# The projections of a Mamba block as one pipeline over 128 blocks in written order

## The chip, the cores and the metric

The kernel runs on one core of one Trainium2 chip. A core has five engines with queues of their own: TensorE (PE, with its weight loads shown as PEld), VectorE (DVE), ScalarE (ACT), GpSimd (POOL) and SyncE (SP), which issues the transfers between the main memory and the on-chip memories. Matmuls write into PSUM, from which ACT and DVE read. The metric is the time of one execution on the device in microseconds (us); a run gives several times and their median counts. One execution is also recorded by the profiler.

## The reference

Input `x` has 2 sequences of 4096 tokens and 512 channels, so 8192 tokens in all. The result is `x + layernorm(mamba(layernorm(x)))`, and onto that once more `x + layernorm(ffn(layernorm(x)))`. Everything is computed in float32. Cut to what matters here:

```python
proj = einsum('blh,ph->blp', x, in_proj_w)            # 512 -> 2048
h_in, gate = split(proj, 2)
u = silu(conv(h_in, conv_w) + conv_b)                 # causal, 4 taps, each channel for itself
ssm = einsum('bli,pi->blp', u, x_proj_w)              # 1024 -> 128 + 16 + 16
ts, Bm, Cm = split(ssm, [128, 144])
dt = softplus(einsum('blr,ir->bli', ts, dt_proj_w) + dt_proj_b)
dA = exp(dt[..., None] * A);  dBx = (dt * u)[..., None] * Bm[:, :, None, :]
hstates = associative_scan(dA, dBx)                   # over the tokens
y = (einsum('blin,bln->bli', hstates, Cm) + D * u) * silu(gate)
return einsum('bli,hi->blh', y, out_proj_w)
```

The feed-forward part multiplies by two weights that are stored in 4 bits with scales per block of 64 and have a low-rank addition (16); between them stands a ReLU.

## The kernel before

The kernel has two stages. Stage A computes the projections of all tokens and prepares the weights of stage B, and writes everything into tensors in the main memory (names ending in `_d`). Stage B runs the scan, the output projection and the feed-forward part. Its instructions on ACT, SP, PE and POOL stand in the order in which they are written out by hand, with a pace of so many matmuls per scan; DVE's are ordered by the framework's scheduler.

**Precision.** A float32 value is held as a high and a low part in the matmul format (`split`: the cast on ACT, the subtraction on DVE), and `mm3` (L99 to L102) makes one product of three matmuls: high x high, high x low, low x high.

**Stage A.** The tokens go in 16 groups of 512 (`g`); the 1024 inner channels in 8 blocks of 128 (`ib`). In stage A before the change all engines are ordered by the framework's scheduler, which lays out a list per engine ahead of time; a few ties are added by hand (`after`, `pace`, `in_set`). What belongs to one group:

- `load_x`, `norm_x`: four tiles of 128 tokens by 512 channels are loaded into the buffers `xA` (4) and normalized on DVE; `rstd_of` takes the power on POOL.
- `turn_x`: four transposes per tile on PE into a PSUM buffer `tp`, then the high part `xnh` on ACT (L174) and the low part `xnl` on DVE (L175). From group 2 on the parts of the last two tiles are stored to `xg_d`, so that stage B can make their gates.
- `h_block`, once per `ib`: twelve matmuls into a PSUM buffer `pm` (two of them, pool `phA`), a copy `hin` on ACT (L335) with three tokens of the group before in front (`halo`, POOL, L334 and L336), the fourth tap on ACT (L337), the other three taps on DVE (L339). In `rest`: silu on ACT into `u` (L344), and the split `us`.
- `gate_block`: twelve matmuls for 128 tokens by 512 gate channels into a PSUM buffer of the pool `psA` (two, which the products `z` of dt and the preparations also use), silu on ACT into `gs` (L361, two buffers), a store to `g_d`. Groups 0 and 1 make eight of these, the later groups the four of their first two tiles; stage B makes the rest in `gates`, from `xg_d` and `wg_d`.
- `x_proj`, once per `ib`: five matmuls with `us`, three blocks behind `h_block`, the last three at the end of the group. Then `x_out` (splits `ts`, stores C) and, in the next group, `b_out` (turns and stores B).
- dt of a group is made during the next one: `dt_mm` (three matmuls, and the bias on ACT or DVE by turns, L400 and L398) in blocks 0 and 1; `dt_out` after block 1: an activation table load, eight softplus (L308) with their stores to `dd_d`, the stores of `du` = D u (L311), the products dt u on POOL (L313), and a table load back; `q_out` in blocks 5 to 7 (2, 3, 3): four transposes of a product into a PSUM buffer `qt` (pool `ptA`, two, which `tp` also uses), a split into `qs` (two buffers of each part) and two stores to `dT_d`.
- Three preparations of weights (`prep_out`, `prep_ffn`): load, dequantize on DVE with the low-rank product from PE, split on DVE and POOL (L184, L185), two stores.

Ahead of the groups the input weights are loaded and split in one row (`load_w`, L244 to L251): sixteen tiles of the input projection, eight of x_proj, two of dt.

After the last group, dt of group 15 is made alone in a sixteenth turn of the loop with no other projections.

**The order of stage B's start.** Its first units need dt, B, C and q of the first group only; its loads stand on SP in the written order.

## Time and profile before

| what | us |
|---|---|
| median of 3 runs | 4846.12 |
| lowest and highest run | 4838.14, 4855.83 |
| the profiled execution, time | 4849.73 |
| the profiled execution, span | 4847.9 |
| PE busy | 4563.9 (94%) |
| DVE busy | 3836.7 (79%) |
| ACT busy | 3320.0 (68%) |
| POOL busy | 3272.9 (68%) |
| mean granted PE clock | 0.977 |

The span is the time from the first to the last instruction of the profiled execution; busy times are shares of it. Matmuls overlap one another, so PE can be shown busy and still not be at its peak: starts of neighbouring matmuls tell more than durations. Lines name an instruction by engine and line of the program, and by the tile it writes and those it reads; "idle before" is the time that the engine stood before it, and behind the arrow is what ended it. Stage A takes roughly the first 1100 us, stage B the rest.

### The profile page before, as it was taken

What the parts mean: (1) busy time and instruction counts of PE and PEld (TensorE: products, weight loads), DVE (VectorE), ACT (ScalarE), POOL (GpSimd) and SP (SyncE); (2) the same over time, 40 slices, a digit from 0 to 9 for tenths busy, and PEclk for the clock granted to TensorE, in tenths of its full rate; (3) what the DMA queues carried; (4) which work ended last, traced back from release to release, by engine and by line L of the source; (5) the groups of instructions that cost most, each with busy time, mean ns of one, the idle gap of its engine ahead of it and who ended that gap; (6) DMA issues with size and microseconds to landing.
All of it is one profiled execution on the core that took longest, in us unless ns stands there. A gap on an engine that the chain in (4) does not pass through costs nothing.

```text
span 4847.9 us, 85729 instructions
## 1 busy us (share of the span) xinstructions
PE 4563.9 (94%) x26736; PEld 3920.6 (81%) x26736; DVE 3836.7 (79%) x6307; ACT 3320.0 (68%) x7411; POOL 3272.9 (68%) x2327
## 2 busy tenths in 40 slices
PE   8999999977999999999999999999999999999999
PEld 6766676756788888888888888888888888888877
DVE  6666666657787898898989888888989898898931
ACT  5766666776777767777676776667776767676643
POOL 2223323227787888888888878888888888788820
PEclk9999999988999999999999999999999999999999
DMA  6877777666798878878787867787787878878765
GB/s 204 244 220 230 218 219 225 214 190 181 225 252 242 235 216 239 229 225 240 213 250 219 240 181 228 216 237 228 225 239 214 250 218 239 225 226 233 215 216 195
DMA packets 1145393, 1085.15 MB, mean 224 GB/s; under 512 B 147281, under 2 KB 918865, under 8 KB 1144946
## 3 DMA queue, kind: packets, MB, share of 16 engines
q1 hardware_dynamic: 1144946, 1079.68, 76.3%
q8 instruction: 221, 3.62, 0.3%
q14 instruction: 226, 1.85, 0.1%
HBM read 801.99 MB, written 277.36 MB: 223 GB/s over the span
## 4 chain that ended last, share of the span: by engine, by line
PE 72%; DMA 12%; DVE 6%; ACT 4%; issue 2%; SPq 2%; POOL 1%; DVEq 0%; ACTq 0%; POOLq 0%
PE yp L711 16%; PE b L661 8%; PE pu L100 5%; PE pu L101 5%; PE pu L102 5%; PE fa L100 5%; PE fa L101 5%; PE fa L102 5%; DMA ys<-y_d 3%; DMA d<-dT_d 2%; DVE pm L339 2%; PE pm L100 2%; DVE h L679 2%; PE pm L101 2%; PE pm L102 1%
## 5 line engine op out<-in xcount | busy, mean ns | idle before, releaser
L691 POOL TENSOR_TENSOR pr<-h,cb 128x1008 f32<-128x1008 f32 (+1 forms) x1056 | 2451.5, 2333 | 525.6 <-DVE b L678 240.2
L679 DVE TENSOR_TENSOR_SCAN h<-dA,b 128x512 f32<-128x512 f32 x2080 | 2534.9, 1220 | 150.0 <-ACT dA L635 15.4
L635 ACT ACTIVATE dA<-dt,A 128x252 f32<-128x252 f32 (+1 forms) x4352 | 1763.5, 487 | 171.8 <-DVE h L679 150.4
L711 PE MATMUL yp<-ident,pr 128*126 128x128 f32 (+1 forms) x8448 | 1114.4, 276 | 17.9 <-POOL pr L691 7.9
L711 PEld LDWEIGHTS yp<-ident,pr 128*126 128x126 f32 (+1 forms) x8448 | 961.4, 141 | 25.4 <-POOL pr L691 9.3
L661 PEld LDWEIGHTS b<-bd,d 128*128 128x128 f32 x4160 | 759.0, 191 | 202.8 <-DMA d<-dT_d 24.1
L661 PE MATMUL b<-bd,d 128*128 128x256 f32 x4160 | 875.8, 292 | 44.9 <-DMA d<-dT_d 22.3
L995 ACT ACTIVATE pu<-pu,bu 128x512 f32<-128x512 f32 x256 | 168.8, 659 | 680.7 <-PE pu L102 680.6
L339 DVE SCALAR_TENSOR_TENSOR pm<-hin,cw,pm 128x512 f32<-128x512 f32 x384 | 284.9, 750 | 233.7 <-ACT pm L337 218.5
L100 PE MATMUL pu<-xh,wu 128*128 128x512 f32 x960 | 411.3, 428 | 58.9 <-DMA wu<-wu_d 58.9
L100 PE MATMUL fa<-wn,hh 128*128 128x512 f32 x1024 | 421.4, 411 | 0.0
L101 PE MATMUL fa<-wn,hh 128*128 128x512 f32 x1024 | 403.7, 394 | 0.0
L102 PE MATMUL fa<-wn,hl 128*128 128x512 f32 x1024 | 401.2, 392 | 0.0
L678 DVE COPY b<-h 128x8 f32<-128x8 f32 x1536 | 255.0, 166 | 178.4 <-PE b L661 170.4
L101 PE MATMUL pu<-xl,wu 128*128 128x512 f32 x960 | 386.4, 402 | 0.0
L102 PE MATMUL pu<-xh,wu 128*128 128x512 f32 x960 | 384.2, 400 | 0.0
L999 DVE TENSOR_TENSOR hl<-pu,hh 128x512 fp32r<-128x512 f32 x256 | 171.8, 671 | 158.4 <-ACT hh L997 158.4
L559 POOL TENSOR_TENSOR bd<-dl,bp 128x512 fp32r<-128x512 f32 x260 | 270.6, 1051 | 11.1 <-DMA d<-dT_d 11.1
L336 POOL COPY halo<-hin 128x3 f32<-128x3 f32 x128 | 31.8, 249 | 331.8 <-ACT hin L335 331.8
L313 POOL TENSOR_TENSOR v<-v,u 128x512 f32<-128x512 f32 x128 | 167.9, 1343 | 124.9 <-DMA dd_d<-v 86.2
L100 PEld LDWEIGHTS pu<-xh,wu 128*128 128x128 f32 x960 | 184.9, 193 | 79.0 <-DMA wu<-wu_d 57.4
L102 PEld LDWEIGHTS fa<-wn,hl 128*128 128x128 f32 x1024 | 192.3, 188 | 44.9 <-DVE hl L999 0.6
(554 smaller groups left out, 7825.1 us busy)
## 6 DMA issues: line engine op xcount, KB each, us to landing
d<-dT_d SPq DMA_DIRECT2D x1024, 128.0 KB
wu<-wu_d SPq DMA_DIRECT2D x256, 512.0 KB
wn<-wn_d SPq DMA_DIRECT2D x256, 512.0 KB
cb<-C_d SPq DMA_DIRECT2D x128, 512.0 KB
wo<-wo_d SPq DMA_DIRECT2D x128, 512.0 KB
dd_d<-du SPq DMA_DIRECT2D x128, 256.0 KB
dd_d<-v SPq DMA_DIRECT2D x128, 256.0 KB
ys<-y_d SPq DMA_DIRECT2D x128, 256.0 KB
```

Of the source, the lines that this page charges most:

```text
L100: nc.tensor.matmul(ps, ah, bh, start=start, stop=False)
L101: nc.tensor.matmul(ps, ah, bl, start=False, stop=False)
L102: return nc.tensor.matmul(ps, al, bh, start=False, stop=stop)
L339: cv = nc.vector.scalar_tensor_tensor(pm, hin[:, k:k + G], cw[:, ib, k:k + 1], pm, ALU.mult, ALU.add)
L559: nc.gpsimd.tensor_mul(tb, dl.unsqueeze(1).to_broadcast([P, N, 32]), bp[:, w // 2, w % 2, :].unsqueeze(2).to_broadcast([P, N, 32]))
L635: nc.scalar.activation(dA[2 * (k % 2) + hf][:, :n_, m, 1:U], dtv, AF.Exp, scale=A[:, ib, n:n + 1])
L661: nc.tensor.matmul(b[:, :, v * 32:(v + 1) * 32], t4[:, u, v, :], Bd[2 * u + v][:, hf * NH:(hf + 1) * NH, :], start=True, stop=True)
L678: nc.vector.tensor_copy(b[:, :, 0], hs["prev"][:, hf])
L679: scans.append(nc.vector.tensor_tensor_scan(h[:, uu].rearrange("p n t -> p (n t)"), dAt[:, u].rearrange("p n t -> p (n t)"), b.rearrange(" ...
L691: nc.gpsimd.tensor_mul(to, h[:, :uu + 1, :, f:], Cb[j, hf][:, :uu + 1, :, f:])
L711: nc.tensor.matmul(yp[:m], pr[:, n, :m], ident, is_transpose=True, start=(hf == 0 and n == 0), stop=False)
L999: nc.vector.tensor_sub(hl, pu, f32(hh))
```

## The change

Stage A gets one loop over 128 blocks (16 groups of 8), and its instructions on ACT, SP, PE and POOL now stand in the written order, as in stage B. DVE remains with the scheduler. In a block, in this order:

- the twelve matmuls of this block (`h_mm`); silu and split of the block before (`h_rest`); what was put off from the block before (`dq`: subtractions and stores of `q_out`, pieces of the normalization); copy and taps of this block (`h_conv`), and `halo_in` of the next block; `du_out` of the block before; weight loads of the first group (`brought`);
- dt of the group before: two `dt_mm` ahead of x_proj and two behind it, in blocks 2 and 3, with all bias additions on ACT; in block 4 a table load, eight softplus with their stores, a table load back; POOL's products by `MPL` in blocks 4 to 7 (1, 3, 2, 2); `q_out` by `QPL` in blocks 6, 7 and the next 0 (3, 3, 2);
- gates by `GPL` in blocks 0, 4, 6 and 7 (group 0: two in each of 4 to 7; group 1: one in each);
- in block 7 the turning of the next group's tiles into the one pair `xnh`, `xnl`, those tiles first that no gate still reads;
- `x_proj` of two blocks before, over the border of groups, so that a group's last two come in blocks 0 and 1 of the next; `x_out` in block 1, `b_out` in block 2;
- preparations by `WPL` (work in blocks 1, 5, 6) and `LPL` (loads in blocks 1 and 5).

The input weights beyond the first four tiles are loaded, in group 0, block by block; the copies `wg_d` are stored in blocks 8 to 15. The buffers of `u` become 12 (from 10), those of `us` 2 (from 3). The last group makes all of its eight gates in stage A, four of them behind its last block beside the start of its dt, and stage B's lists of gates and its pace leave that group out.

```diff
-        if '0' == '1':
-            sa.enter_context(tc.manual_schedule(engines={mybir.EngineType.PE}))
+        sa.enter_context(tc.manual_schedule(engines=ENG_A))
...
-        up = sa.enter_context(tc.tile_pool(name="uA", bufs=10))
+        up = sa.enter_context(tc.tile_pool(name="uA", bufs=12))
...
+        for b_, f, args in [(0, load_wi, (1, 0)), (0, load_wi, (1, 1)), (1, load_wi, (1, 2)), (1, load_wi, (1, 3))] + [
+                (1 + k // 3, load_wx, (k,)) for k in range(KI)] + [
+                (3 + k // 2, load_wi, (2 + k // 4, k % 4)) for k in range(8)] + [
+                (7, load_wd, (k,)) for k in range(2)] + [(8 + k, store_wg, (k // 4, k % 4)) for k in range(8)]:
+            brought.setdefault(b_, []).append((f, args))
...
+            qh = p3.tile([P, J, P], FR, name=f"qs_{g}_{ib}h", tag="qsh")
+            nc.scalar.copy(qh, qt)
+
+            def rest():
+                ql = p3.tile([P, J, P], FR, name=f"qs_{g}_{ib}l", tag="qsl")
+                nc.vector.tensor_sub(ql, qt, f32(qh))
+                for k, t in enumerate((qh, ql)):
+                    nc.sync.dma_start(dT_d[ib, g * G:(g + 1) * G].rearrange("(j p) k i -> k p j i", p=P)[k], f32(t))
+
+            dq.append(rest)
...
-            if ib % 2:
-                nc.vector.tensor_scalar_add(vv, z, db[:, ib:ib + 1])
-            else:
-                nc.scalar.activation(vv, z, AF.Identity, bias=db[:, ib:ib + 1])
+            nc.scalar.activation(vv, z, AF.Identity, bias=db[:, ib:ib + 1])
...
+        QPL = (2, 0, 0, 0, 0, 0, 3, 3)
+        MPL = (0, 0, 0, 0, 1, 3, 2, 2)
+        WPL = (0, 1, 0, 0, 0, 1, 1, 0)
+        LPL = (0, 2, 0, 0, 0, 1, 0, 0)
...
+            if st:
+                h_mm(g, st, ib)
+            if b:
+                h_rest((b - 1) // KI, last, (b - 1) % KI)
+            while dq:
+                dq.pop(0)()
+            if st:
+                h_conv(g, st, ib)
+                if b + 1 < KI * NG:
+                    halo_in(*divmod(b + 1, KI))
+            if b:
+                du_out((b - 1) // KI, last, (b - 1) % KI)
+            for f, args in brought.pop(b, []):
+                f(*args)
...
+                ng = GPL.get(g, (1, 0, 0, 0, 1, 0, 1, 1))[ib]
+
+            if ib in (2, 3) and old:
+                for i in range(2):
+                    dt_mm(g - 1, old, 4 * ib - 8 + i)
+            if ib == 7 and st and g + 1 < NG:
+                rest = {j for j, _ in st["gates"]}
+                for j in range(J):
+                    if j not in rest:
+                        turn_x(g + 1, st["xt"], j)
+            if ib in (4, 6, 7) or g < 2:
+                for _ in range(ng):
+                    gate(g, st, fs)
+                ng = 0
+            if ib == 7 and st and g + 1 < NG:
+                for j in range(J):
+                    if j in rest:
+                        turn_x(g + 1, st["xt"], j)
+            if ib == 4 and old:
+                switch("softplus")
+                for i in range(KI):
+                    soft(g - 1, old, i)
+                switch("silu_and_others")
+            for f in fs:
+                f()
+            fs = []
+            if b >= 2:
+                x_proj((b - 2) // KI, old if ib < 2 else st, (b - 2) % KI)
+            if ib == 1 and old:
+                x_out(g - 1, old)
+            if ib == 2 and old:
+                b_out(g - 1, old)
+            if ib in (2, 3) and old:
+                for i in range(2, 4):
+                    dt_mm(g - 1, old, 4 * ib - 8 + i)
+            for _ in range(ng):
+                gate(g, st, fs)
+            if g:
+                for _ in range(WPL[ib]):
+                    if loaded:
+                        loaded.pop(0)()
+            for _ in range(QPL[ib]):
+                if qm:
+                    q_out(*qm.pop(0))
...
+        for i in range(KI + 3):
+            if i == 1:
+                switch("softplus")
+            if i < KI:
+                dt_mm(NG - 1, old, i)
+            if i == 0:
+                b_out(NG - 1, old)
+            if 1 <= i <= KI:
+                soft(NG - 1, old, i - 1)
+            if 2 <= i <= KI + 1:
+                times_u(NG - 1, old, i - 2)
+            if i >= 3:
+                q_out(NG - 1, i - 3, old["v"][i - 3])
+                while dq:
+                    dq.pop(0)()
...
-            todo_ = [(g, j) for g in range(GS, NG) for j in range(JS, J)]
+            todo_ = [(g, j) for g in range(GS, NG - 1) for j in range(JS, J)]
```

## The prediction

> **What bounds the kernel now.** I read, in this order: busy time by stage (core 0: length, busy time of PE, PEld, DVE, ACT and POOL with instruction counts, granted PE clock, DMA share, GB/s), the groups of instructions by shape in the first 1111 us, the waits, the chain that ended last, and PE's and ACT's instructions in order of time.

> ```profile
> 22.00:88.00 66.00, 64.30 (x272) 50.49 (x273) 46.70 (x87) 37.19 (x66) 13.49 (x25) 1.00 0.73 240
> 157.00:1002.00 845.00, 776.69 (x3535) 588.47 (x3534) 558.91 (x942) 556.57 (x937) 247.50 (x359) 0.97 0.74 222
> 1044.00:1111.00 67.00, 30.89 (x135) 21.31 (x134) 25.98 (x34) 49.50 (x126) 20.23 (x21) 0.67 0.61 173
> 1111.00:1319.00 208.00, 180.02 (x1149) 160.17 (x1147) 170.00 (x281) 154.11 (x358) 169.54 (x108) 0.94 0.74 212
> ```

> The projections end near 1111 us; the change is nearly all before that. PE is the fullest engine there, though not full. Every eighth hin copy marks a group: 31.4, 88.1, 156.9, 216.5 ... 943.8, 1001.5 us. Groups 2 to 14 take 844.6 us, 65.0 each, in turns of about 62.5 and 69.5. Matmuls of 512 columns start 0.229 us apart and transposes 0.11, so a steady group's 208 matmuls (47.6), 52 transposes (5.7) and three preparations (1.7) are 55 us: 10 of the 65 are stalls and slow clock.

> ```profile
> 290.94 6.99 DMA dd_d<-v
> 297.99 6.41 DMA g_d<-gs
> 304.50 0.61 ACT gs L361
> 305.15 1.22 PE pw_0p L223
> ```

> The chain names the odd groups' stall: burst of softplus stores, gate store, gate buffer, PE (3.8 us).

> ```profile
> 335.27 0.39 PE L324 MATMUL bc<-us_6l,Wb 128*64 128x512 f32 x1
> 337.54 0.69 PE L172 MATMUL tp<-ident,xt 128*128 128x128 f32 x4 [1.88 <-DVE qs_6l L96]
> ```

> ```profile
> 335.00:338.00 3.00, 1.12 (x8) 0.60 (x6) 2.48 (x3) 1.93 (x3) 1.87 (x2) 1.00 0.80 224
> 338.00:341.40 3.40, 3.35 (x11) 1.95 (x10) 3.35 (x6) 1.32 (x3) 1.05 (x1) 0.51 1.04 323
> ```

> PE's rows and the stretches around them show the other kind: transposes that wait for a PSUM buffer, and then 3.4 us at clock 0.51.

> ```profile
> L339 DVE SCALAR_TENSOR_TENSOR pm<-hin,cw,pm 128x512 f32<-128x512 f32 x384 | 284.9, 750 | 233.7 <-ACT pm L337 218.5 <-POOL v L313 8.5 <-POOL hin L334 2.5
> L311 ACT ACTIVATE du<-u,Ds 128x512 f32<-128x512 f32 x128 | 93.0, 726 | 0.0
> L308 ACT ACTIVATE v<-v 128x512 f32<-128x512 f32 x128 | 69.7, 618 | 0.2
> L298 ACT ACT_TABLE_LOAD x32 | 41.1, 1283 | 0.6
> ```

> ```profile
> 530.91 0.58 ACT L95 CAST qs_6h<-qt 128x512 fp32r<-128x512 f32 x1 [0.62 <-DMA dT_d<-qs_4h]
> ```

> ```profile
> SPq L312 <- ACT du L311: 102.9, 64, 6.3
> ```

> Durations to carry on: conv step 0.75, du 0.73, softplus 0.62 (0.52 apart), table load 1.28; a store of q issued at 528.05 freed its buffer at 530.91, 2.9 us later; SP already waits for du.

> **The change, part by part** (own time 4849.7: span 4847.9 and 1.8 around it; 3.6 above the median).

> *Steady groups, x13.* PE's work stays 55 us by count. ACT takes over 64 v adds (0.69 against 0.75 on DVE); its per-group sum is 50 us, some 44 with the 0.1 by which its instructions overlap. Both fit in 65, so what counts is order: ACT, PE, POOL and SP now wait in program order, and what stands behind a waiting instruction waits too. Start block 4's matmuls at 0:
> - Softplus. hin, pm, du end at 4.7; load 1.28, eight softplus 5.5 to 10.3, load to 11.6, gate silu to 12.1, silu of block 4 to 12.8. PE is through blocks 4 (29 matmuls, 6.6) and 5 (4.4) at 11.0, and block 6 needs block 4's pm buffer: stall 1.9. Silu also needs one of 12 u buffers, freed by POOL's multiply after the softplus store: 6.6+3.3+1.3=11.2, in time; if the store takes the chain's 7, 2.8 more (left out of the sum, held by its upper end).
> - Three q_out in block 6, with two qt and two qs buffers. The third transposes wait for the first's subtraction behind conv: 1 to 2. Its copy on ACT waits for the first's store, which SP issues behind the preparation's stores (DVE, then POOL 1.29), at 23 to 25 plus 2.9. ACT stands 4 to 6 us, the next silu and hin behind it.
> - turn_x right after block 7's matmuls. The second transpose waits for the third q's buffer: 0 to 3. The third needs xnh and xnl of the first: ACT must pass silu, us, hin, pm, du first (3.2 us), then copy 0.59 and subtract 0.68 beside conv: 2.5 to 4.5.
> - The third q_out of block 7: 0.8; dt in blocks 2 and 3: 0.4.

> Gone: the gate-buffer stall above. Sum 6.6 to 12.6, and slow clock. The row at 338.0 halves the clock for 3.4 us after some 2 us of idleness, 1.7 us lost; I take one such stretch a group, between none and two (3.4). So 6.6 to 16 of stalls, 61.6 to 71 a group; I take 10.5, between the steps' middle (9.6 + 1.7 = 11.3) and the 10 of today's rows, whose waits are of the same kinds: 65.5, 13 x 0.5 = +6, ends 13 x (-3.4) = -44 and 13 x 6 = +78.

> [...]

> *Group 0.* Loads of later weights, now ahead in SP's queue, move behind each block's du store (du waits for ACT, 4.7 into a block), and ACT's casts behind their landing (two issues 0.43 each, 2.9 to land, cast 0.62). That is about 4 us of ACT per block over its 3.6, so blocks 1 to 3 take 7.8 instead of 2.7 to 3.9. Blocks 4 and 6 use, in their gates, tiles that they load themselves: 6.5 of PE each. From 22.5: block 4 at 54, 5 at 76, 6 at 86, 7 at 102, 8 at 113, against 85 now (hin at 88.1 less 3). I take +25 of these 28 (some casts are DVE's); ends 0 (all landed in time, as now) and +30.

> *Group 1.* Eight gates, as now, one per block: 24+24 more matmuls than a steady group (11 us), stalls 6: 72 against 68.8, +3 (-3 to +8). The 16 wg_d stores move here on SP, 16 x 0.45 = 7 us in which SP has only waits to lose; price 0, up to 4 inside that range.

> *Last group and tail.* Now the last group runs from 998.6 to the last q transposes at 1087.7, 89 us. Then: 55, then two x_proj, four gates (48 matmuls, 11.0) and q_out, 15, then dt, softplus, multiply, q in turn: store 3.3, POOL 1.34, transposes, dt, v, softplus is 7.3 us per three blocks, 2.4 each, some 25 in all. 95, +6 (-10 to +12). Today four scans run inside the tail (1061 to 1079) and the fifth comes at 1099, some 11 behind the last q; behind the new tail all wait for its end, which at 1.65 a scan (208 us for 126) is 7 at most and lies inside the upper end.

> *Scan stage.* Two gate tiles less in each of two stretches: 48 x 0.229 = 11 at most. PE is busy 180 of 208 there, not all of it; -7 (-11 to 0).

> *The small edits, at nothing together.* Halo copies a block ahead (0.19 on POOL) and its memset moved from DVE to POOL: POOL is idle 70% of these groups; without that cover 128 x 0.19 = 24 us would stand before conv. Normalization in three pieces on DVE, which is 66% busy and loses 64 x 0.75 of v adds: its pieces run two blocks ahead of their use. x_proj two blocks behind instead of three: in a block of 4.4 us conv and silu need 2.8+1.3+2.3+1.3 = 7.7 us, and x_proj comes more than 8 after its block's start; were it late, 1 us in two blocks of a group. The last group's four xg_d stores and loads go and four gate stores come, on an SP that waits for ACT there anyway.

> Sum: +25 +3 +6 +6 -7 = +33: 4849.7 + 33 = 4883 in a profiled execution, 4879 as a median.

> **The rivals.**
> - *Faster:* the third q's store is issued early and the turns overlap, so that steady groups lose 5 us, a group is 60. For it: even groups lose 6.3 today, and the 3.8 us gate stall with its clock goes. Against: the softplus stall of 1.9 and the third transpose's 2.5 follow from the order alone, and the DMA share of 0.74 would have to rise to 0.80 with latencies no longer. 13 x (-5) +27 = -38: 4808. It decides below 62.9 a group.
> - *Worse:* ACT's standstill reaches the next group's first blocks and the clock halves twice: 70 a group, +65+27: 4938. For it: SP's row of 102.9 us behind du; against: blocks 0 and 1 leave ACT room.
> - *No change:* weights land in time (group 0 +2) and groups take 65: 4846 to 4850. Against: SP cannot issue them before du.

> [...]

> **How the numbers follow.** Forecast (slower by 10 to 60) 0.44, worse 0.13, no change 0.09, faster 0.34. 0.3% is 15 us, what a measurement of this kernel can tell. Faster 0.34, same 0.09, slower 0.57. The forecast's own range is 4860 to 4910; over the cases, from the faster one with its other terms favourable (4795) to the worse one (4935).

> **What would show it.** Hin copies of blocks 8 apart: 65.5 in steady groups. PE idle at h_mm of block 6 ended by ACT's u, and at the second and third tp by DVE's xnl or qs; clock 0.5 after it. ACT idle before the third q copy, ended by dT_d. Block 8 at about 110, PE idle in group 0 ended by Wil. The last qt some 95 after the last group's start. Groups near 60, or group 0 below 70 us, would make the forecast wrong.

## The result and the profile after

The changed kernel takes 5037.5 us (median of 4 runs, 5023.8 to 5043.3), the kernel before 4850.6 (4 runs, 4838.1 to 4855.8). The ratio is 1.0385, with a 95% interval of 1.0354 to 1.0417: 187 us slower, where the prediction had 4879 as a median, 4860 to 4910 as the forecast's own range and 4935 as the upper end over all its cases. The direction was right, the size was not.

The profiled execution of the changed kernel has a span of 5022.1 us, 174.2 more than that of before. The hin copies, marked as in the prediction, put the difference in its place:

| part | before | after | difference | predicted |
|---|---|---|---|---|
| start to the first hin copy | 31.4 | 25.7 | -5.7 | in group 0's |
| group 0 | 56.7 | 87.2 | +30.5 | +25, with the start |
| group 1 | 68.8 | 79.8 | +11.0 | +3 |
| groups 2 to 14, each | 65.0 | 74.9 | +9.97 | +0.5 |
| the thirteen together | 844.6 | 974.2 | +129.6 | +6 |
| last group's first hin to the last q transposes | 86.2 | 111.5 | +25.3 | +6 |
| from there to the end | 3760.2 | 3743.7 | -16.5 | -7 |

Three quarters of the loss lie in the steady groups. The busy times by stage after (length; busy time of PE, PEld, DVE, ACT and POOL with counts; granted PE clock, DMA share, GB/s; the rows are group 0, groups 3 to 14, the last group with its tail, and the first scans):

```profile
22.00:113.00 91.00, 67.64 (x249) 49.88 (x249) 43.13 (x81) 37.31 (x72) 10.61 (x24) 0.85 0.29 86
263.00:1167.00 904.00, 754.81 (x3282) 576.47 (x3281) 511.85 (x831) 543.10 (x913) 212.57 (x335) 0.91 0.64 194
1167.00:1279.00 112.00, 83.47 (x366) 64.01 (x364) 43.57 (x62) 81.32 (x146) 24.82 (x37) 0.84 0.57 167
1279.00:1487.00 208.00, 166.55 (x1058) 148.58 (x1059) 160.09 (x262) 151.44 (x377) 162.81 (x110) 0.90 0.73 198
```

In the steady row no engine is fuller than before: PE's share fell from 0.92 to 0.83, the clock from 0.97 to 0.91, the DMA share from 0.74 to 0.64. Everybody waits more. Nor did the instructions of these groups in stage A become longer: a conv step takes 0.754 us (0.750 before), du 0.722 (0.726), softplus 0.618 (0.618), a table load 1.283 (1.283). Their rows show the waits ahead of them:

```profile
L352 DVE SCALAR_TENSOR_TENSOR pm<-hin,cw,pm 128x512 f32<-128x512 f32 x384 | 289.4, 754 | 101.6 <-ACT pm L350 92.9 <-POOL halo L349 0.6
L319 ACT ACTIVATE du<-u,Ds 128x512 f32<-128x512 f32 x128 | 92.4, 722 | 6.7 <-DMA dd_d<-du 6.5
L311 ACT ACTIVATE v<-v 128x512 f32<-128x512 f32 x128 | 69.2, 618 | 0.2
L306 ACT ACT_TABLE_LOAD x31 | 39.8, 1283 | 0.6
L295 ACT CAST qs_2h<-qt 128x512 fp32r<-128x512 f32 x16 | 9.3, 584 | 106.7 <-DMA dT_d<-qs_0h 100.6 <-PE tp L171 6.0
```

The last row is new: sixteen casts of 0.58 us, with 106.7 us of idle ACT ahead of them. That is the third q of each group. ACT around it in one steady group (start, duration, instruction, idle time and what ended it):

```profile
538.19 0.59 ACT L295 CAST qs_0h<-qt 128x512 fp32r<-128x512 f32 x1
538.65 0.61 ACT L295 CAST qs_1h<-qt 128x512 fp32r<-128x512 f32 x1
548.78 0.58 ACT L295 CAST qs_2h<-qt 128x512 fp32r<-128x512 f32 x1 [9.52 <-DMA dT_d<-qs_0h]
549.26 0.69 ACT L357 ACTIVATE u<-pm,cb 128x512 f32<-128x512 f32 x1
```

The chain of waits through the same place says why (start, duration, what):

```profile
542.82 1.29 POOL pw_0q L183
...
544.12 0.32 SPq L186
...
544.53 4.15 DMA dT_d<-qs_0h
...
548.78 0.04 ACT qs_2h L295
```

The first q was copied by 538.8, but SP issued its store only at 544.5, behind a preparation's two stores, the second of which waited for POOL's subtraction. Then 4.15 us until the buffer was free. PE's stalls in the same group:

```profile
526.28 0.50 PE L101 MATMUL pm<-xnh,Wih 128*128 128x512 f32 x1 [1.88 <-ACT u L357]
539.96 0.63 PE L293 MATMUL qt<-ident,v 128*128 128x128 f32 x4 [3.08 <-DVE qs_0l L299]
550.25 1.11 PE L171 MATMUL tp<-ident,xt 128*128 128x128 f32 x4 [4.88 <-DVE qs_2l L299]
553.95 1.11 PE L171 MATMUL tp<-ident,xt 128*128 128x128 f32 x4 [2.59 <-DVE xnl L174]
```

These are the four places that the prediction named.

The group shown, group 6, has the longest of these waits. In the other groups from 3 to 13 the store is also issued 5.75 us after the copy, but frees its buffer some 2.7 us later. In group 14, in which no preparation's store stands ahead of it, it is issued at once, and ACT stands 2.6 us. These are the third copy in groups 7 and 14, and the store in the chain of group 7:

```profile
624.45 0.58 ACT L295 CAST qs_2h<-qt 128x512 fp32r<-128x512 f32 x1 [7.95 <-DMA dT_d<-qs_0h]
...
1151.13 0.59 ACT L295 CAST qs_2h<-qt 128x512 fp32r<-128x512 f32 x1 [2.61 <-DMA dT_d<-qs_0h]
```

```profile
621.76 2.59 DMA dT_d<-qs_0h
```

SP's own waits over groups 3 to 14 are these (total, count, longest):

```profile
SPq L320 <- ACT du L319: 150.8, 61, 6.9
SPq L371 <- ACT gs L370: 76.7, 36, 6.2
SPq L186 <- DVE pw_1h L182: 45.2, 16, 4.0
SPq L186 <- DVE pw_0h L182: 42.9, 16, 4.0
```

### The profile page after: what moved, and what is told of

The parts are those of the page before. It is cut to its first block, busy times and chain, and to the rows that moved or that the text cites. A ratio compares the mean times of both kernels' runs of the same rounds, so it can differ in the third digit from the quotient of the medians.

```text
span 5022.1 us, 85593 instructions
## 1 busy us (share of the span) xinstructions
PE 4607.4 (92%) x26736; PEld 3957.7 (79%) x26736; DVE 3814.4 (76%) x6241; ACT 3358.2 (67%) x7471; POOL 3248.0 (65%) x2329
## 3 DMA queue, kind: packets, MB, share of 16 engines
q1 hardware_dynamic: 1142258, 1076.53, 74.9%
## 4 chain that ended last, share of the span: by engine, by line
PE 69%; DMA 11%; ACT 6%; DVE 6%; issue 4%; POOL 2%; SPq 2%; POOLq 0%; DVEq 0%; ACTq 0%
PE yp L802 15%; PE b L752 8%; PE pu L101 5%; PE pu L102 5%; PE pu L103 5%; PE fa L101 5%; PE fa L102 5%; PE fa L103 5%; DMA ys<-y_d 2%; DVE h L770 2%; DVE pm L352 2%; DMA d<-dT_d 1%; DMA wu<-wu_d 1%; PE pm L101 1%; PE pm L102 1%
## 5 line engine op out<-in xcount | busy, mean ns | idle before, releaser
L101 PE MATMUL pm<-xnh,Wih 128*128 128x512 f32 x512 | 222.1, 434 | 30.9 <-ACT u L357 30.3
```

The source lines that it names most:

```text
L101: nc.tensor.matmul(ps, ah, bh, start=start, stop=False)
```

## The experiments

Theory A: ACT stands before the third copy of q until the first one's store has gone out, and what SP has in front of that store sets the length. Theory B: the turn of the next group's tiles stalls by the written order on ACT, whatever q does. Theory U: the u buffers, a stall that the prediction named and left out. The measure is the mean of groups 2 to 14 by their hin copies. The changed kernel gave 74.9; e4 and e8, whose steady groups have the same code, gave 75.5 and 75.8, so a difference below 1 us a group is not read. Most kernels here ran once, e10, e14 and e15 twelve times. None of them leaves out a part of the work.

**e1_q2: q by twos.** No block has a third q.

```diff
-        QPL = (2, 0, 0, 0, 0, 0, 3, 3)
+        QPL = (2, 2, 0, 0, 0, 0, 2, 2)
```

> Products of dt are turned two per block, in blocks 6, 7, 0 and 1, instead of 3, 3 and 2 (the end of the loop stores after each one). Theory A (the third copy of a block stands on ACT until the first one's store has landed, and carries its delay into the next block's silu, hin, turn_x and into the clock): a steady group falls from 74.9 us to 65 to 68, PE's waits between transposes of q from 5.0 us a group to under 1, half-clock time from 12.9 us a group to 5 or less. Theory B (turn_x is what costs: its third tile waits for the first one's parts behind silu, us, hin, pm and du on ACT, whatever q does): a steady group stays at 71 to 74 and only the 5.0 between q's transposes shrinks.

4967.4 us, 70.8 a group. The stall between q transposes went (5.0 us a group before). A part came back at block 6's matmuls, which wait for ACT's silu: over groups 3 to 14 that wait (total, count, longest; first the changed kernel, then this run) grew from 2.0 to 5.1 us a group.

```profile
PE pm L101 <- ACT u L357: 23.5, 12, 4.4
...
PE pm L101 <- ACT u L357: 61.0, 12, 7.5
```

The third q is worth 4 us a group, not the whole loss, and the group lies just above A's span and just below B's.

**e2_prep: another place for the preparations.**

```diff
-        WPL = (0, 1, 0, 0, 0, 1, 1, 0)
+        WPL = (0, 1, 1, 0, 0, 1, 0, 0)
```

> The preparation worked in block 6 is worked in block 2 instead, so its two stores no longer stand on SP ahead of q's. Theory A with SP's order as the main part (q's first store was ready at 538.8 and issued at 544.5 us in group 6): the third copy starts some 5 us earlier and a steady group falls from 74.9 to 68 to 71. If the store's own landing (about 4 us) is the main part, or under theory B: 73 to 75.

5040.9 us, 76.6 a group. ACT's wait before the third copy fell from 7.5 to 4.4 us a group, but PE's wait ahead of dt's matmuls rose from 0.4 to 3.2, and groups now alternate between about 72 and 85. Moving the preparation's work bought one wait with another. This run doesn't separate the theories.

**e3_sp_free: SP ordered by the scheduler.**

```diff
-    ENG_A = ENG
+    ENG_A = {getattr(mybir.EngineType, e) for e in ['Activation', 'PE', 'Pool']}
```

> SP's instructions in the first stage are ordered by the scheduler again, the three other engines stay in written order. If SP's written order is the main cause (stores of q behind preparations, weight loads behind stores of du): group 0 falls from 87.2 to 60 to 70 and steady groups from 74.9 to 68 to 71. If ACT's and PE's written order is (theory B, or the landing alone): group 0 falls by under 5 and steady groups stay at 73 to 76.

4950.3 us, 70.3 a group, group 0 in 72.5 (from 87.2). ACT's wait before the third copy fell to 2.7 us. SP's written order costs some 5 us in each group and 15 in group 0.

**e4_load: the weights in one row ahead of block 0.**

```diff
+        for kt in range(KH):
+            load_wi(1, kt)
...
-        for b_, f, args in [(0, load_wi, (1, 0)), (0, load_wi, (1, 1)), (1, load_wi, (1, 2)), (1, load_wi, (1, 3))] + [
...
+        for b_, f, args in [(8 + k, store_wg, (k // 4, k % 4)) for k in range(8)]:
```

> All input weights are loaded and split in one row ahead of the blocks, as before the change; everything else as in the changed kernel. If the first group's 87.2 us come from loads that SP issues only behind each block's store of du: first group 57 to 64, first hin copy no more than 8 us later, the other groups unchanged, in all 20 to 28 us less. If they come from the written order of silu, hin and du: first group above 75.

5015.7 us. Group 0 takes 57.7, 29.5 less, nearly all that it had lost. The first hin copy comes at 36.4, 10.7 later, so from the start to the end of group 0 the edit gains 18.8, and the last q is 10 us earlier. So the loads behind du were group 0's cost. The waits of the changed kernel's group 0 show both halves of it, SP behind du and ACT's cast and the gate's matmuls behind the weights:

```profile
SPq L320 <- ACT du L319: 42.4, 7, 12.6
```

```profile
ACT Wih L248 <- DMA wl<-in_in_wT: 19.9, 5, 5.0
...
PE pg L101 <- DVE Wih L248: 14.3, 3, 5.0
```

**e5_mul: POOL's products earlier.**

```diff
-        MPL = (0, 0, 0, 0, 1, 3, 2, 2)
+        MPL = (0, 0, 0, 0, 4, 2, 2, 0)
```

> One list of numbers changes: POOL makes four of the eight products in block 4 of the next group, two each in blocks 5 and 6 (MPL 4, 2, 2, 0 in blocks 4 to 7), instead of 1, 3, 2, 2, so that the u buffers that blocks 5 to 7 wait for come free before the preparation's subtraction on POOL. Theory U (the u buffer, which the prediction named and left out of its sum): ACT's silu no longer waits for POOL in blocks 5 to 7 (5.7 us a group in the changed kernel), the stall at block 6's matmuls of 1.8 us goes and some of the clock with it, 72 to 73 us a group, 35 us in all. Theory A (what sets the pace is ACT's standstill before the third copy of q): ACT only arrives there earlier and stands longer, 74.5 to 75.5 a group, within 10 us of the changed kernel.

5045.0 us, 75.9 a group. Silu's wait for POOL's products, 68.8 us over twelve groups in the changed kernel (first line), is gone. In its place silu waits for the conv (69.6 us, against 21.8), and ACT stands 9.3 us a group before the third copy instead of 7.5 (the other lines):

```profile
ACT u L357 <- POOL v L315: 68.8, 12, 6.2
...
ACT qs_2h L295 <- DMA dT_d<-qs_0h: 106.5, 11, 13.5
ACT u L357 <- DVE pm L352: 69.6, 24, 5.6
```

Theory U falls: silu did wait for its buffer, where the prediction had it free in time, but ending that wait gained nothing, so leaving it out of the sum was right.

**e6_turn: the gate between the second and the third turn.**

```diff
-                for j in range(J):
-                    if j not in rest:
-                        turn_x(g + 1, st["xt"], j)
+                first = [j for j in range(J) if j not in rest]
+                for j in first[:2]:
+                    turn_x(g + 1, st["xt"], j)
...
-                for j in range(J):
-                    if j in rest:
-                        turn_x(g + 1, st["xt"], j)
+                for j in first[2:] + sorted(rest):
+                    turn_x(g + 1, st["xt"], j)
```

> In block 7 the gate's twelve matmuls (2.75 us) move from between the third and the fourth tile's transposes to between the second and the third, so that PE has work while ACT comes to the first tile's copy. Theory B (the turn waits for ACT's written order): the stall of 2.9 us at the third tile goes, with the clock behind it; 71.5 to 73 us a group, 25 to 45 us in all. Theory A (ACT arrives late because of the copy of q it stood at in block 6): the second tile's stall of 5.0 us stays and the gate fills only part of what follows; 74 to 75, 0 to 12 us.

4988.6 us, 71.9 a group. PE's rows in one group: the second turn still waits for the third q, the third and fourth come without a wait (eight transposes in a row).

```profile
534.72 1.12 PE L171 MATMUL tp<-ident,xt 128*128 128x128 f32 x4 [3.29 <-DVE qs_2l L299]
540.75 1.08 PE L171 MATMUL tp<-ident,xt 128*128 128x128 f32 x8
```

So A and B each hold for a part, at different places.

**e7_all: q by twos, SP by the scheduler, the products of e5, and the gate as in e6.**

```diff
+    ENG_A = {getattr(mybir.EngineType, e) for e in ['Activation', 'PE', 'Pool']}
...
+        QPL = (2, 2, 0, 0, 0, 0, 2, 2)
+        MPL = (0, 0, 0, 0, 4, 2, 2, 0)
...
+                for j in first[2:] + sorted(rest):
```

> Four edits together: q in blocks 0, 1, 6, 7 by twos, SP ordered by the scheduler, products 4, 2, 2, 0, the gate between the second and third turn. If the causes lie side by side, the single savings add: 4.1 (q by twos) + 4.7 (SP) and 2 to 3 each of the other two where they hold, 61 to 64 us a group, 4850 to 4890 in all, near the kernel before. If they are one and the same standstill seen at different places, the group falls no further than to 67 to 69, 4910 to 4940.

4845.4 us, 63.0 a group. The single savings of e1, e3 and e6 (4.1, 4.7, 3.1) add to 11.9, and the four edits together save 11.9. With SP left to the scheduler they lie side by side; e9 below shows that with SP in the written order they do not.

**e8_lastg: the last group's four gates back in the scan stage**, with its list, its pace and its stores as before.

```diff
-        GATES.get(g, GATES[1][:2 * JS] if g < NG - 1 else GATES[1])
+        GATES.get(g, GATES[1][:2 * JS])
...
-            todo_ = [(g, j) for g in range(GS, NG - 1) for j in range(JS, J)]
+            todo_ = [(g, j) for g in range(GS, NG) for j in range(JS, J)]
```

> The last group's four gates of its last two tiles go back to the scan stage (its list, its pace and the stores of xg_d as before); all else as changed. By the prediction's step the gates cost 11 us in the tail (48 matmuls at 0.229) and save 7 to 11 in the scan stage: last group and tail 111.5 to 100, scan stage 3744 to between 3751 and 3755, total within 5 us of the changed kernel. If the tail's excess over the predicted 95 is the chain of dt, softplus, store, product and q, which the gates only lie beside, the tail keeps 107 to 111 and the kernel is 5 to 15 us slower. If the 16.5 us that the scan stage gained are not the gates', it stays at 3744 and the kernel is up to 11 faster.

5044.6 us. Last group and tail fall from 111.5 to 101.9, the scan stage rises from 3743.7 to 3761.5. In single executions, then, moving the gates costs 9.6 and saves 17.8. The other runs tell how much of this is firm. Over the fifteen profiled executions with the gates moved, last group and tail take 109 to 114 us and the scan stage 3735 to 3757, 3745 in the mean; the two with the gates in the scan stage (this run and the kernel before) have 102 and 86 us, then 3762 and 3760. Both shifts are clear of the spread. Their sum is not: 3863 here, 3846 to 3865 in the fifteen. That moving the gates is a gain is not shown. Nearly 16 us of the tail's 25 are not the gates'.

**e9_q2_turn: e1 and e6 together, SP written.**

```diff
+        QPL = (2, 2, 0, 0, 0, 0, 2, 2)
...
+                for j in first[2:] + sorted(rest):
```

> q in blocks 0, 1, 6, 7 by twos and the gate between the second and the third turn; SP stays in the written order, products and loads as changed. Alone the edits saved 4.1 and 3.1 us a group, with SP left to the scheduler and other products all four 11.9. If the causes lie side by side, 74.9 - 4.1 - 3.1 = 67.5 to 68 us a group, 4920 to 4940 in all, and SP's written order still costs some 4.7 a group and 15 in group 0. If with twos the third copy's wait is gone and with it what SP's order cost in the steady groups, 63 to 65, 4870 to 4895.

4954.0 us, 69.8 a group. The two edits save 5.1 together where they saved 7.2 one by one, so here they don't add: block 6's matmuls now wait 4.0 us a group and dt's 3.3 (groups 3 to 14: total, count, longest).

```profile
PE pm L101 <- ACT u L357: 48.4, 12, 5.5
PE z L101 <- DVE pw_0s L223: 18.2, 6, 4.7
PE z L101 <- DVE pw_1s L223: 16.0, 5, 4.6
```

With no third q in any block, SP's order still costs 6 (against e10 below). In the group that starts at 530 us the du made at 548.6 was stored only at 559.5, behind the preparation's and q's transfers on SP; ACT stood from 562.96 to 566.88 for its buffer, and softplus, for which block 6's silu waits, began only behind that.

**e10_best: q by twos, the gate of e6, SP by the scheduler, the loads of e4** (12 executions).

```diff
+    ENG_A = {getattr(mybir.EngineType, e) for e in ['Activation', 'PE', 'Pool']}
...
+        for kt in range(KI):
+            load_wx(kt)
...
+        QPL = (2, 2, 0, 0, 0, 0, 2, 2)
...
+                for j in first[2:] + sorted(rest):
```

> The four edits without the change of the products (these again 1, 3, 2, 2), and all weights loaded in one row ahead. The loads saved 10 us between start and last q when they were moved alone; with SP free already group 0 may gain only what lies between 73 and 58 less the 10.7 later start, 5. If the products are worth nothing (as alone): 63 us a group, 4830 to 4845, faster than the kernel before by 0.1 to 0.5%. If they matter once the other stalls are gone (ACT's silu stands for POOL), 65 to 67, 4860 to 4890, slower than it.

4859.1 us against 4856.7 on the same chip, ratio 1.0007 (0.9994 to 1.0021): the kernel before's time. 64.0 a group, between the two cases, and 1 us above e7, whose products are the earlier ones; a difference of that size is at the limit of what single profiles tell.

**e11_pool_free: the same with POOL by the scheduler too.**

```diff
-    ENG_A = {getattr(mybir.EngineType, e) for e in ['Activation', 'PE', 'Pool']}
+    ENG_A = {getattr(mybir.EngineType, e) for e in ['Activation', 'PE']}
```

> As the kernel with the products as changed and the loads ahead, but POOL too is ordered by the scheduler, so only ACT and PE stand in the written order. If POOL's order is what silu still waits for (the preparation's subtraction and the power ahead of the products), 61 to 63 us a group, 2 below the one with POOL written; if not, the two are within 1 us a group.

4838.9 us, 62.9 a group, 1.1 below the one with POOL written, so neither case is clearly met.

**e12_pst: only the preparations' stores move**, behind the next block's stores of q and du; SP stays written.

```diff
-                nc.sync.dma_start(d.rearrange("p k c -> p (k c)") if up_ else d, f32(t))
+                pst.append((d.rearrange("p k c -> p (k c)") if up_ else d, f32(t)))
...
+            while pst:
+                nc.sync.dma_start(*pst.pop(0))
             for f, args in brought.pop(b, []):
```

> SP stays in the written order; only the stores of the preparations move: they are issued a block later, behind that block's stores of q and of du, and no longer between them and the store that the third copy of q waits for. If what SP's order costs is the place of these stores (theory A as the prediction named it: SP issues the first q's store behind the preparation's), the groups fall as with SP left to the scheduler, to 70 to 71 from 74.9, 4965 to 4980 in all (group 0's loads stay). If it is SP's other waits (du's store, the gate's), 73.5 to 75, 5005 to 5040.

4958.8 us, 70.7 a group, what SP by the scheduler gave. SP and ACT in one of its groups: the first q's store follows 1 us after its copy, and ACT stands 5.5 us, in the mean 4.2 instead of 7.5.

```profile
520.94 0.59 ACT L297 CAST qs_0h<-qt 128x512 fp32r<-128x512 f32 x1
...
527.54 0.59 ACT L297 CAST qs_2h<-qt 128x512 fp32r<-128x512 f32 x1 [5.52 <-DMA dT_d<-qs_0h]
```

```profile
522.49 0.62 SPq L303 DMA_DIRECT2D dT_d<-qs_0h  x1
```

**e13_pst_q2_turn: e12 with q by twos and the gate of e6.**

```diff
+                pst.append((d.rearrange("p k c -> p (k c)") if up_ else d, f32(t)))
...
+        QPL = (2, 2, 0, 0, 0, 0, 2, 2)
...
+                for j in first[2:] + sorted(rest):
```

> The same with q by twos and the gate between the second and the third turn. These two alone left 69.8 us a group with SP written and 64 with SP by the scheduler (loads and products aside). If the preparations' stores are what SP's order still costs there (the softplus burst starts late behind a du store that stands behind them), 64 to 66 a group, 4880 to 4905. If it is other waits of SP, 68.5 to 70, 4935 to 4955.

4873.7 us, 64.7 a group with all four engines still in the written order. In the steady groups, written order as such is not what costs; three places in it are. The kernel is still 32 us above the 4841.8 of the kernel before beside it, 24 by the profiled executions. Those 24 are group 0's: it takes 88.1, 31 more than before, 7 of which come back by the earlier start; the last group's +27 and the scan stage's -25 nearly cancel.

**e14_pool_free_again and e15_pool_free_mul: e11 again (12 executions), and with the products of e5 (12).** The edit of e15 against e14:

```diff
-        MPL = (0, 0, 0, 0, 1, 3, 2, 2)
+        MPL = (0, 0, 0, 0, 4, 2, 2, 0)
```

> The kernel with POOL and SP by the scheduler, q by twos, the gate between the turns and the loads ahead, timed against the kernel before: one execution gave 4839, with 62.9 us a group against 65.0. If that holds, 0.3 to 0.5% faster than before (ratio 0.995 to 0.997); if the single time was on the low side of the spread of 0.3%, the same within 0.2%.

> The same with the products 4, 2, 2, 0 in blocks 4 to 6. Alone that list saved nothing, with SP free and q by twos the group was 63.0 with it and 64.0 without. If the u buffers are a stall of their own once the others are gone, 61.5 to 62.5 us a group and 10 to 15 us below the kernel without it, some 0.6% faster than before; if POOL, free to choose, already makes the products early enough, within 5 us of it.

4833.3 and 4833.4 us against 4841.8: ratios 0.998 (0.9967 to 0.9994) and 0.9983 (0.9971 to 0.9995). With only ACT and PE in the written order they are 0.2% below the kernel before, the intervals just clear of 1, with 63.0 and 62.7 a group. The products are worth nothing here either.

## Why the prediction was too low

**The steady groups** were built up from the right parts: 55 us of PE work, stalls, and slow clock, 65.5 in all. Measured in the changed kernel, gaps of over 0.25 us between matmuls, each counted as 0.231 us (512 columns) or 0.110 (fewer), mean of groups 2 to 14:

| step of the prediction | predicted | measured |
|---|---|---|
| softplus, block 6's matmuls | 1.9 | 2.2 |
| third q's transposes (block 6) | 1 to 2 | 3.8 |
| second turn | 0 to 3 | 3.0 |
| third turn | 2.5 to 4.5 | 2.8 |
| last q (block 7) | 0.8 | 1.1 |
| dt | 0.4 | 0.7 |
| all stalls, with 1.2 at other places | 6.6 to 12.6, 8.8 taken | 14.9 |
| slow clock, and gaps below 0.25 us | 1.7 | 74.9 - 55 - 14.9 = 5.0 |

The same count gives 7.4 of stalls and 2.5 of slow clock and small gaps in the kernel before, so of the 10 us that a group lost three quarters are stalls and one quarter is clock and small gaps. The gate-buffer stall went, as predicted.

The step that failed is the third q, with what it hands on to the second turn: "ACT stands 4 to 6 us", and 1 to 5 us of PE's standing at the two places. ACT stood 7.5 us in the mean, up to 9.5, and PE 6.8. The prediction had the mechanism, to the queue and the transfer, and it had the store's landing (2.9 us, measured 2.7 in nine of the groups 3 to 13). What it put too early is the time at which SP issues the store: it comes 5.75 us after the copy. The e12 run shows this: with nothing moved but the preparations' stores, ACT's wait falls to 4.2, into the predicted span, and the group by 4.2 us. The other term that was mis-sized is the clock, 1.7 us against 5.0, below.

Taking 65.5 although the steps' upper end was 71 made the miss larger; it leaned towards "the 10 of today's rows, whose waits are of the same kinds". That the scheduler's list had placed such waits beside other work, while a written order passes each on to what stands behind it, is a reading that no run isolates. How far the stalls add up depends on what else is written: with SP left to the scheduler the single savings of e1, e3 and e6 add (e7), with SP written those of e1 and e6 give 5.1 of 7.2 (e9), and with the preparations' stores moved as well all three give 10.2 of 11.4 (e13).

**The clock** was put at one half-speed stretch of 3.4 us a group, up to two. There were 3.8 (12.9 us of half clock a group; 4.5 before the change, 3.7 in e7). Granted clock and PE's work in five neighbouring stretches of 3.41 us of the changed kernel:

```profile
544.20:547.63 3.43, 1.17 (x7) 0.76 (x6) 0.00 (x0) 0.00 (x0) 2.34 (x2) 1.00 0.97 314
547.63:551.04 3.41, 0.79 (x4) 0.71 (x4) 1.09 (x2) 2.23 (x5) 0.00 (x0) 0.50 0.93 256
551.04:554.45 3.41, 0.82 (x5) 0.50 (x4) 2.95 (x6) 2.21 (x5) 2.76 (x4) 0.50 0.62 195
554.45:557.87 3.42, 3.42 (x11) 2.74 (x10) 1.40 (x3) 0.59 (x1) 0.00 (x0) 0.50 0.82 236
557.87:561.28 3.41, 3.41 (x21) 2.68 (x20) 0.69 (x1) 1.11 (x3) 0.00 (x0) 1.00 0.17 50
```

The first three, in which PE is busy for 1.17, 0.79 and 0.82 us, are each followed by one at half clock, the fourth, in which it is busy throughout, by one at full clock. The fourth itself stands at 0.50 though full of work: its matmuls start 0.43 us apart instead of 0.23. So the price of these stalls is not their length: two of 4.88 and 2.59 us, 3.7 us apart (550.25 and 553.95), go with three stretches of half clock.

**Group 0** came out as built: the prediction counted from the kernel's start, and by that count it is +24.8 for +25 (hin of group 1 at 112.9 instead of 88.1), by the cause named (e4, e3). **Group 1**, +11 for +3, exceeds its bound of +8. It was 78.5 in e6 and 73.1 in e1, but 70.0 with both edits (e9), so nearly all of the excess is what the steady groups have too, the third q and the turn.

**The last group and tail** missed by 19. Where, the starts of PE's instructions tell: from the last group's first hin to its last block 49 us where some 52 were said (55 less the 3 ahead of the hin copy), from there to dt's first matmul 21 for 15, and from there to the last q 41 for 25. The step that failed is thus the chain of dt, softplus, product and q, "2.4 each, some 25 in all". In the changed kernel its softplus take turns with the first scans' exponentials, with two loads of activation tables of 1.28 us at every turn, nine between 1239 and 1265:

```profile
1252.78 0.63 ACT L311 ACTIVATE v<-v 128x512 f32<-128x512 f32 x1
1253.42 1.28 ACT L726 ACT_TABLE_LOAD   x1
1254.72 2.01 ACT L726 ACTIVATE dA<-dt,A 128x63 f32<-128x63 f32 x8
...
1258.27 1.28 ACT L311 ACT_TABLE_LOAD   x1
1259.57 0.63 ACT L311 ACTIVATE v<-v 128x512 f32<-128x512 f32 x1
```

In e8 the scans' exponentials come ahead of the chain, four loads stand there, and the chain takes 30. So the 9.6 that e8 took off the tail are not the gates' matmuls alone, and the nearly 16 that stayed are not these turns. Against the kernel before, 8 of them lie in the last group's blocks (49 for 41) and 8 in the chain (30 for 22); why is open. An order without the turns and with the gates was not tried.

**The scan stage** gained 16.5 where 11 was the bound. By e8 the gain is the gates' (17.8). But fifteen executions of the same code took 3735 to 3757, so a true gain of 11 is not excluded.

Of the rivals, "Worse" came nearest: ACT's standstill and a clock that halves more than once are what happened, with 70 us a group as its price where 75 was measured (its sum is 4938, and the range ends at 4935, slightly below it). That the standstill reaches the next group's first blocks is not what happened: PE has no gap of over 0.6 us in blocks 0 and 1 of the steady groups.

## What to carry to other kernels

When an engine's queue goes from a scheduler's list to a written order, price a wait not by its own length but by what stands in front of the instruction that ends it, on that instruction's queue: here a store of 0.4 us of issue stood 6 us behind two others on SP, and a cast of 0.6 us on ACT held everything behind it. Two buffers used three times in a row, and a step that needs a result of the engine behind whose queue it stands, are the places to look for; each could be mended by a few lines without giving up the order (64.7 us a group with all four engines written). And when several such stalls lie at different places, count on nearly their sum (it ranged here from 5.1 of 7.2 to all of 11.9), and look at the granted clock behind each: here a window of half clock, 3.413 us, followed every full-clock window of the steady groups in which PE idled for 2.25 us or more.

## What was not expected of the hardware

What goes ahead of a half-clock window came out sharper than the prediction's "some 2 us of idleness". These are counts from the clock records and PE's rows of the profiled executions: over the steady groups of all the sixteen kernels (e11 and e14 are one), windows of 3.413 us on the grid, idleness being the time not covered by matmuls at 0.231 (512 columns) and 0.110 us (fewer; at full clock the median distances of starts in the changed kernel's steady groups are 0.230 and, for transposes, 0.109):

| this window | idle | next at half clock | next at full clock |
|---|---|---|---|
| full clock | below 1.25 us | 0 | 3097 |
| full clock | 1.25 to 2.25 | 77 | 336 |
| full clock | 2.25 and more | 244 | 0 |
| half clock | below 2.0 | 1 | 321 |
| half clock | 2.0 and more | 170 | 0 |

The kernel before and the changed one alone give, in the order of the rows, 0 and 381, 8 and 46, 30 and 0, 0 and 38, 28 and 0. Stalls of like length came out differently: in the changed kernel one of 1.88 us (ended at 526.28) lay within one window and the next was granted 0.50, one of 2.24 us (ended at 228.55) lay across the border of two, at 226.78, and both of these and the next were granted 1.00. Also, the profiled execution of the changed kernel was 13.7 us below the median of its runs, and kernels with the same steady code differed by 0.9 us a group: a single profile of these kernels tells a group's time to about 1 us.
